# Two graph layers on one core: last 256 columns of e turned by VectorE, last products by halves, tie counts from one scan

## The chip, the cores and the metric

The kernel runs on one core of a Trainium2 chip. Its metric is the device time of one execution in microseconds (us), as the median of three runs. A core has TensorE (PE in the profile; its weight loads are listed as PEld), VectorE (DVE), ScalarE (ACT), GpSimd (POOL) and SyncE (SP), which here issues nearly all DMAs. Each engine executes its own instructions in the order in which they were issued and waits at semaphores for the others.

## The reference

`x` is 3327 x 256, `adj` is 3327 x 3327, everything in float32. Two residual layers are computed.

Layer 0 takes `h = relu(layernorm(x))` and makes two steps (n = 0, 1) with a dense graph and a learned one:

```
R  = (adj + I), rows scaled to sum 1
Xf = Xa = Z0 = h;  Z = 0
for n in (0, 1):
    q, k = Xa W1' W2', Xa W3'
    p = softmax(q k')                      # 3327 x 3327
    A = p, of each row the largest entries until 0.9 of the sum is reached;
        the rest is zero; rows scaled again to sum 1
    Xf = R Xf;  Xa = A Xa
    Z += Xf U1[n]' + Xa U2[n]'
x = x + layernorm(h + Z)
```

Entries that are equal at the border of the 0.9 are kept in the order of their columns. Layer 1 is a graph attention with four heads of 64: `hp = relu(layernorm(x)) W`, scores `leaky_relu(s_i + d_j)` where `adj[i, j] > 0`, softmax over j, product with `hp`, then `x + elu(...)`.

## The kernel before

The 3327 nodes are padded to 26 tiles of 128 (NT = 26, NP = 3328). The whole program is written as pieces of work given to a planner, the class `Plan`. Each piece has an engine, a length in us, a rank (smaller is sooner), the pieces that it needs, and counted buffers that it takes and gives back; `lag` is the time after its end at which others may build on it, for a DMA the time to landing. `Plan.order` simulates the engines with these lengths and lags and writes the instructions out in that order. So a changed length, lag or buffer count changes no computation, but can change the order of issue on every engine.

One **row tile** of attention (52 of them: 26 in each step) goes like this. `logits` (L905) makes q k' in PSUM in pieces of 1024, 1024, 1024 and 255 columns; `exps` (L920) is ScalarE's exponential of each piece into the buffer `e` (128 x 3328). `count` (L959) counts on ScalarE against trial thresholds and GpSimd steps them. `window` (L1017, L1022) takes on VectorE the best eight of each of 16 column pieces as 128 candidates; `sort` and `choose` (L1049 to L1070) find the smallest value kept, and how many entries equal to it are kept: `choose` marks the ties among the candidates (L1062), sums them over the four quarters of the row (L1064, L1065), scans the four sums (L1066), and makes one threshold for each quarter (L1069, L1070). `drop` (L1075) zeroes what lies under the threshold, quarter by quarter: 1024, 1024, 1024 and 255 columns.

The product A Xa needs the tiles of `e` transposed. In 49 of the 52 rows (`BLOCKED`) the first three quarters take this way: `turn_blocks` (L1112) transposes 32 x 32 blocks on VectorE, `put_blocks` (L1116) writes the quarter to DRAM, `get_blocks` (L1121) reads it back in four DMAs with the blocks in their places, and `attend_blocks` (L1128) multiplies eight tiles of it with `rhs` on TensorE. `exps` writes these quarters with pairs of tiles interleaved, for that purpose. The last two tiles, columns 3072 to 3327, are transposed by two TensorE matmuls with the identity (`turn`, L1087) into a PSUM buffer of the pool `px`, copied to SBUF by ScalarE or VectorE (L1098), and multiplied from there (`attend`, L1105). In the other three rows, at the end of step 1, all 26 tiles go that second way. There are two `px` buffers, shared with the projections of `finish1` and `finish2`. Beside the rows, `Full` multiplies adj with main or c (L1153), from tiles `at` that SP loads (L1147): in both steps this fills TensorE between the rows.

**Layer 1** (`attend_neighbours`) is four column blocks b of W = 832 nodes, each over the 26 source tiles j. For every j ScalarE makes a mask (L1751, L1752), VectorE makes four heads of 832 exponents (L1763) in a buffer `e` or `e2`, TensorE makes the products (`product`, L1779, 128 x 64 weights, two heads beside each other) and the denominators (`sums`, L1793, 128 x 32 weights, four heads beside each other); `sums` of two j are put together (`JG = 2`). When the last j is through, ScalarE copies the sums out of PSUM (L1842, L1848), and for each of seven tiles TensorE transposes (L1866), VectorE divides (L1904, L1905), ScalarE makes relu and exp (L1914, L1915), GpSimd adds x (L1918), VectorE joins (L1922) and SP stores (L1925). In the last block nothing else is left to do beside this.

Of the kernel before, what the change touches and what calls it, by code (L numbers as in the profile page):

```python
# [587 lines left out]
def fast(  # L588
# [58 lines left out]
    with ExitStack() as l0:  # L647
# [23 lines left out]
        blocks = spill.tile([3, 4, P, 2 * P], F32, name="blocks")  # L671
# [194 lines left out]
        plan = Plan(dict(rows=1, mvs=3, pl=2, px=2, acca=1, accf=1, et=3, at=4, y=1, e2=3, mask=2, e5=1, qg=2, **BUFS))  # L866
# [4 lines left out]
        class Row:  # L871
# [3 lines left out]
                "b w t0 t1 t2 u g k2 p0 p1 p2 p3 D0 D1 D2 v z r0 s0 s1 s2 h x th tq mid dh kh fl d up h0 h1 room zs cnt "  # L875
# [38 lines left out]
            def exps(self, k):  # L914
                pl = self.pl.pop(k)
                to = self.e[:, PART * k : PART * k + pl.shape[1]]
                if k < 3 and self.i < BLOCKED[self.n]:
                    to = to.rearrange("p (g q t) -> p g t q", g=4, t=2)
                    pl = pl.rearrange("p (g t q) -> p g t q", g=4, t=2)
                S.activation(  # L920
                    to,
                    pl,
                    AF.Exp,
                    accum_out=(self.p0, self.p1, self.p2, self.p3)[k],
                )

            def row_sum(self):
                k = self.NAMES.index("p0")
                S.activation(self.sc[:, k + 4 : k + 8], self.sc[:, k : k + 4], AF.Copy, accum_out=self.s)
# [114 lines left out]
            def choose(self):  # L1044
# [14 lines left out]
                V.scalar_tensor_tensor(out_, win, nxt, keep, ALU.is_gt, ALU.mult, accum_out=self.cnt)  # L1059
                V.tensor_sub(self.m, met[:, 2, i], self.cnt)  # L1060
                ties = small.tile([P, PIECES * 8], F32, name="rest", bufs=1).rearrange("p (c r) -> p c r", r=8)
                V.tensor_scalar(ties, self.cands, nxt, None, ALU.is_equal)  # L1062
                num, upto = (small.tile([P, 4], F32, name=name, bufs=1) for name in ("num", "upto"))
                V.tensor_reduce(num[:, :3], ties[:, :15, :].rearrange("p (a c) r -> p a (c r)", a=3), AX.X, ALU.add)  # L1064
                V.tensor_reduce(num[:, 3:], ties[:, 15, :], AX.X, ALU.add)  # L1065
                V.tensor_tensor_scan(upto, num, num, 0.0, ALU.add, ALU.bypass)  # L1066
                V.scalar_tensor_tensor(num, upto, self.m, num, ALU.is_le, ALU.mult, accum_out=met[:, 4, i])
                self.thr = small.tile([P, 4], F32, name="thr")
                V.tensor_scalar(upto, upto, self.m, 2.0**-24, ALU.is_gt, ALU.mult)  # L1069
                V.tensor_scalar(self.thr, upto, 1.0 - 2.0**-24, nxt, ALU.add, ALU.mult)  # L1070

            def drop(self, o):

                piece = self.e[:, o * PART : min((o + 1) * PART, N)]
                V.scalar_tensor_tensor(piece, piece, self.thr[:, o : o + 1], piece, ALU.is_gt, ALU.mult)  # L1075
# [24 lines left out]
            def attend(self, g):  # L1100
# [3 lines left out]
                for j in range(4 * g, min(4 * g + 4, NT)):  # L1104
                    T.matmul(  # L1105
                        self.acc, et[:, j - 4 * g, :], rhs[self.n][:, j, :], start=(j == 0),
                        stop=j == NT - 1 and self.i >= BLOCKED[self.n],
                    )

            def turn_blocks(self, g):  # L1110
                part = self.e[:, g * PART : (g + 1) * PART].rearrange("p (g s t) -> p g t s", g=4, t=2)
                V.transpose(part, part)  # L1112

            def put_blocks(self, g):
                src = self.e[:, g * PART : (g + 1) * PART].rearrange("p (g w) -> p g w", g=4)
                nc.sync.dma_start(blocks[g].rearrange("g p w -> p g w"), src)  # L1116

            def get_blocks(self, g, o):
                part = slice(o * P // 4, (o + 1) * P // 4)
                src = blocks[g, :, :, o * P // 2 : (o + 1) * P // 2].rearrange("g (b s) w -> s (g b) w", b=4)  # L1120
                nc.sync.dma_start(self.e[part, g * PART : (g + 1) * PART].rearrange("p (c w) -> p c w", w=P // 2), src)  # L1121

            def attend_blocks(self, js, stop):
                for j in js:
# [3 lines left out]
                    T.matmul(self.acc, lhs, rhs[self.n][:, j, :], start=(j == 0), stop=stop and j == js[-1])  # L1128
# [180 lines left out]
        def finish1(row, done, rank):  # L1309
# [73 lines left out]
            y = plan.put("SP", 0.5, r + 0.3, store, needs=[a], give=["ystage"], lag=3.0)  # L1383
# [97 lines left out]
        def failures(n):  # L1481
# [14 lines left out]
            V.tensor_tensor(one, met[:, 4], met[:, 5], ALU.not_equal)  # L1496
# [7 lines left out]
        def search(row, rank, keys, stats_of, fresh):  # L1504
# [4 lines left out]
            for g in range(2):  # L1509
# [8 lines left out]
                for k in (2 * g, 2 * g + 1):  # L1518
                    got.append(
                        plan.put("ACT", 1.15 if k < 3 else 0.5, rank - 2.5, row.exps, k, needs=[a], give=["pl"])  # L1520
# [29 lines left out]
            a = plan.put("DVE", 3.1, rank - 1.0, row.choose, needs=[a, may], take=["cum"])  # L1550
            total = plan.put("POOL", 1.0, rank - 1.0, row.total, needs=[a], give=["cum"])
            drops = []
            for o in range(4):
                a = plan.put(
                    "DVE", 1.07 if o < 3 else 0.4, rank - 1.0, row.drop, o, needs=[a], hold=1.0 if o < 3 else 0.3,
                    lag=0.15 if o < 3 else 1.5,
# [4 lines left out]
        def attention(row, rank, total, drops, right):  # L1561
            a = None
            if row.i < BLOCKED[row.n]:
                come = []
                for g in range(3):
                    b = plan.put("DVE", 1.25, rank - 1.001, row.turn_blocks, g, needs=[drops[g]])
# [5 lines left out]
                last = plan.put("PE", 0.22, rank - 0.01, row.turn, 6, needs=[drops[3]], take=["px"])  # L1572
                last = plan.either(
                    ("ACT", 0.27, row.turned_by_s), ("DVE", 0.39, row.turned_by_v), rank - 2.6, 6, needs=[last],
                    take=["et"], give=["px"],
                )
                for j in (0, 4, 8, 12, 24, 16, 20):
                    if j == 24:
                        a = plan.put("PE", 0.864, rank, row.attend, 6, needs=[last, a], give=["et"])
                        continue  # L1580
                    a = plan.put(
                        "PE", 1.728, rank, row.attend_blocks, range(j, j + 4), j == 20, needs=[come[j // 8], a, right],
# [19 lines left out]
        def full(n, t, rank, right, after):  # L1602
# [3 lines left out]
                plan.put("SP", 0.4, rank, f.load, q, needs=[after], take=["at"], lag=3.3) for q in range(-(-NT // JC))  # L1606
# [20 lines left out]
        def attend_neighbours(rows, ends, done, fulls):  # L1627
# [4 lines left out]
            JG = 2  # L1632
            logits_done = [r.pieces["logits"] for r in rows]
# [73 lines left out]
            for b in range(4):  # L1707
# [13 lines left out]
                group, groups_e = [], []  # L1721
                for j in range(NT):
# [31 lines left out]
                    def exponents(a, j=j, held=held, b=b):  # L1754
                        if a == 0:
# [3 lines left out]
                                if k < 4  # L1759
                                else extra["e"][k - 4]  # L1760
# [11 lines left out]
                    def product(a, j=j, held=held, q=q, open_acc=open_acc):  # L1772
# [3 lines left out]
                        for c in range(2):  # L1776
# [10 lines left out]
                    def sums(j=j, held=held, q=q, open_den=open_den):  # L1787
# [3 lines left out]
                        for c in range(2):  # L1791
# [14 lines left out]
                    else:  # L1806
# [5 lines left out]
                    mine = "e" if j % 7 < 4 else "e2"  # L1812
                    x_ = plan.put(
                        "DVE", 2.0, rank, exponents, 0, needs=[m_, both[0], ends[j][0], more if mine == "e2" else None,
# [3 lines left out]
                    last_e = y_  # L1818
                    x_ = plan.put(
# [6 lines left out]
                    if len(group) == JG or j == NT - 1:  # L1826
# [22 lines left out]

                r1 = r0 + 9.0  # L1850
# [267 lines left out]
```

## Time and profile before

| | |
|---|---|
| time, median of 3 runs | 2105.58 us (2104.02 to 2105.99) |
| profiled execution: time, span | 2100.08 us, 2098.2 us |
| TensorE busy | 2037.8 us (97%), granted clock 0.994 |
| VectorE busy | 1729.7 us (82%) |
| ScalarE busy | 1300.0 us (62%) |
| GpSimd busy | 990.7 us (47%) |
| DMA | 338.56 MB, 580513 packets; the main queue's packets 66.4% of 16 engines' span |

The profile is of one execution; the span runs from its first to its last instruction. Busy time of an engine is the union of its instructions. A group line of the profile gives source line, engine, operation, output and inputs, shape and count, then busy us, mean ns of one, and the idle time ahead of it with what ended it. float32 matmuls appear as two records each; transposes (L1087) as one. Matmul records overlap, so what one costs is read from start to start. The prologue ends at about 95 us, step 0 of layer 0 at about 750 us with leftovers to 840, step 1 at about 1610 us, and layer 1 fills the rest.

### The profile page before, as it was taken

How to read it: one execution, taken by the hardware profiler on the slowest of the kernel's cores; microseconds unless marked ns; L12 is line 12 of the kernel's file. 1: busy time of each engine (PE TensorE's matmuls, PEld its weight loads, DVE VectorE, ACT ScalarE, POOL GpSimd, SP SyncE). 2: the span in 40 equal slices, each digit the busy share in tenths (PEclk: the TensorE clock that was granted, in tenths of full speed). 3: DMA queues.
4: the chain of work that ended last, by engine and by line, in shares of the span. 5: the costliest groups of instructions: out<-in, count | busy, mean ns of one | idle time of the engine just before them, and what ended most of it. 6: DMA issues, size and time to landing. Idle time of an engine off the chain costs nothing. (4 is left out here: it accounts for less than half of the span.)

```text
span 2098.2 us, 34334 instructions
## 1 busy us (share of the span) xinstructions
PE 2037.8 (97%) x10695; PEld 1415.2 (67%) x10695; DVE 1729.7 (82%) x4105; ACT 1300.0 (62%) x2480; POOL 990.7 (47%) x2170
## 2 busy tenths in 40 slices
PE   8999999999999989989999999999999999999997
PEld 6477777878787778767878787787877333333332
DVE  5689897778876871578998979988987999999895
ACT  5767665666556621777778776778652547465552
POOL 4476654446544630567778777777772000000001
PEclk9999999999999999999999999999999999999999
DMA  4188888678877685697787888887743544453341
GB/s 116 45 190 186 194 180 195 168 152 196 189 183 172 176 186 138 199 232 165 181 189 176 203 188 191 185 191 192 182 126 89 157 141 142 125 147 115 112 127 34
DMA packets 580513, 338.56 MB, mean 161 GB/s; under 512 B 327931, under 2 KB 533281, under 8 KB 580321
## 3 DMA queue, kind: packets, MB, share of 16 engines
q1 hardware_dynamic: 579424, 336.06, 66.4%
q8 instruction: 87, 1.43, 0.3%
q14 instruction: 106, 0.86, 0.1%
q10 hardware_dynamic: 896, 0.21, 0.0%
HBM read 242.86 MB, written 93.05 MB: 160 GB/s over the span
## 5 line engine op out<-in xcount | busy, mean ns | idle before, releaser
L959 ACT ACTIVATE junk<-e,sc 128x3327 fp8e5<-128x3327 f32 x147 | 451.0, 3068 | 31.4 <-POOL sc L996 29.8
L1128 PE MATMUL acca<-rhs,e 128*128 128x256 f32 x1872 | 426.8, 381 | 4.6 <-DMA e<-blocks 4.6
L1128 PEld LDWEIGHTS acca<-rhs,e 128*128 128x128 f32 x1872 | 364.9, 197 | 48.7 <-issue 6.0
L1153 PE MATMUL accf<-c,at 128*128 128x256 f32 x1352 | 316.5, 385 | 17.1 <-DMA at<-in_adjt_dram 8.5
L1153 PE MATMUL accf<-main,at 128*128 128x257 f32 x1352 | 313.3, 381 | 5.4 <-ACT main L1304 2.5
L1153 PEld LDWEIGHTS accf<-c,at 128*128 128x128 f32 x1352 | 252.8, 192 | 67.5 <-DMA at<-in_adjt_dram 10.2
L1153 PEld LDWEIGHTS accf<-main,at 128*128 128x128 f32 x1352 | 250.4, 190 | 54.3 <-issue 11.5
L1022 DVE MAX8 cands<-y 128x8 f32<-128x205 f32 (+1 forms) x832 | 242.9, 361 | 3.6
L1918 POOL TENSOR_TENSOR qq<-qq 128x256 f32<-128x256 f32 x4 | 3.0, 759 | 457.0 <-ACT qq L1914 457.0
L1017 DVE SCALAR_TENSOR_TENSOR y<-e,sc 128x1639 f32<-128x1639 f32 x84 | 165.1, 1965 | 62.9 <-POOL sc L1007 61.7
L920 ACT ACTIVATE e<-pl 128x1024 f32<-128x1024 f32 (+1 forms) x168 | 152.9, 920 | 75.4 <-PE pl L905 74.7
L1752 ACT ACTIVATE et<-at 128x448 bf16<-128x448 f32 (+1 forms) x204 | 112.6, 552 | 128.6 <-DVE e L1763 73.3
L1779 PE MATMUL pl<-e,main 128*64 128x416 f32 x1024 | 190.4, 517 | 0.1
L1075 DVE SCALAR_TENSOR_TENSOR e<-e,thr 128x1024 f32<-128x1024 f32 (+1 forms) x168 | 178.4, 1066 | 2.4 <-DMA at<-in_adjt_dram 0.3
L905 PE MATMUL pl<-kt,qg 64*128 64x512 f32 (+1 forms) x832 | 173.7, 536 | 0.4 <-ACT qq L920 0.4
L1112 DVE STREAM_TRANSPOSE e<-e 128x1024 f32<-128x1024 f32 x117 | 146.1, 1248 | 3.7
L1779 PEld LDWEIGHTS pl<-e,main 128*64 128x64 f32 x1024 | 70.3, 137 | 111.0 <-issue 91.5
L1763 DVE SCALAR_TENSOR_TENSOR e<-c,low,et 128x832 f32<-128x832 f32 x128 | 128.8, 1070 | 6.1 <-issue 3.2
L905 PEld LDWEIGHTS pl<-kt,qg 64*128 64x128 f32 x832 | 71.5, 186 | 83.4 <-issue 76.2
L1751 ACT ACTIVATE at<-at 128x448 f32<-128x448 f32 (+1 forms) x204 | 110.8, 543 | 25.7 <-DMA at<-in_adjt_dram 25.6
L1763 DVE SCALAR_TENSOR_TENSOR e<-qq,low,et 128x832 f32<-128x832 f32 x120 | 120.5, 1073 | 4.1 <-PE accf L1793 2.9
L959 ACT ACTIVATE junk<-qq,sc 128x3327 fp8e5<-128x3327 f32 x35 | 107.4, 3068 | 10.7 <-POOL sc L996 10.4
(550 smaller groups left out, 3540.7 us busy)
## 6 DMA issues: line engine op xcount, KB each, us to landing
at<-in_adjt_dram SPq DMA_DIRECT2D x414, 256.0 KB
blocks<-e SPq DMA_DIRECT2D x117, 512.0 KB
e<-blocks SPq DMA_DIRECT2D x468, 128.0 KB
at<-in_adjt_dram SPq DMA_DIRECT2D x102, 192.0 KB
blocks<-qq SPq DMA_DIRECT2D x30, 512.0 KB
qq<-blocks SPq DMA_DIRECT2D x120, 128.0 KB
at<-in_adjt_dram SPq DMA_DIRECT2D x52, 128.0 KB
ys<-ystage SPq DMA_DIRECT2D x26, 256.0 KB
```

The costliest lines, as they stand in the source:

```text
L905: T.matmul(pl[:, lo : lo + m], qg[self.n, self.i // 4][half, self.i % 4, :], kt[half, 512 * k : 512 * k + m], start=True, stop=True,)
L920: S.activation(to, pl, AF.Exp, accum_out=(self.p0, self.p1, self.p2, self.p3)[k],)
L959: S.activation(junk[:, :N], self.e[:, :N], fn, bias=t, scale=-1.0, accum_out=dst, saturate=False)
L1017: V.scalar_tensor_tensor(self.y[:, : hi - lo], self.e[:, lo:hi], self.up, self.e[:, lo:hi], ALU.is_lt, ALU.mult, accum_out=(self.h0, self. ...
L1022: V.max(self.cands[:, a * PIECES // 2 + k, :], self.y[:, at[k] - lo : at[k + 1] - lo])
L1075: V.scalar_tensor_tensor(piece, piece, self.thr[:, o : o + 1], piece, ALU.is_gt, ALU.mult)
L1112: V.transpose(part, part)
L1128: T.matmul(self.acc, lhs, rhs[self.n][:, j, :], start=(j == 0), stop=stop and j == js[-1])
L1153: T.matmul(self.acc[:, : self.w], self.at[j // JC][:, j % JC, :], self.src[:, j, : self.w], start=(j == 0), stop=(j == NT - 1),)
L1752: S.activation(to, src, AF.Sign)
L1763: V.scalar_tensor_tensor(held["e"][:, k, :], extra["both"][b % 2][:, k, :], low[:, j, k : k + 1], held["mask"], ALU.max, ALU.mult,)
L1779: T.matmul(q["acc"][a][k * FH : (k + 1) * FH, c, :C], main[:, j, h * FH : (h + 1) * FH], held["e"][:, h, c * C : (c + 1) * C], start=(j == 0),
```

## The change

1. The last 256 columns of a blocked row take the way of the first three quarters. The third group becomes 1280 columns wide (10 tiles) in `turn_blocks`, `put_blocks`, `get_blocks`; the two TensorE transposes, their copy and `attend` go. `exps` writes the last piece as two strided halves of 128 and 127 columns, with a fifth sum.
2. `choose` takes the number of kept ties from one instruction, scans the 128 tie marks at once, makes 16 thresholds of which `drop` uses four, and makes the tie check (`met[:, 4]`) behind the thresholds; `failures` reads that check in another form.
3. In the last block of layer 1 the last six j (`LATE`) are multiplied by column halves c of 416: first half 0 of all six, then half 1, with the sums of each half behind its products. `leave_half` copies each half out of PSUM; the tiles that lie in half 0 need only that.
4. In the planner: new lengths, lag 7.0 for 3.0 at the `ys` store and 4.0 for 3.3 at the `at` loads, and the buffer tags `e2=3` become `e2=2, ec=1`, by which j = 0, 7, 14, 21 of layer 1 use the space of `c` and the next four the `e` buffers.

```diff
-        blocks = spill.tile([3, 4, P, 2 * P], F32, name="blocks")
+        blocks = spill.tile([NT // 2, P, 2 * P], F32, name="blocks")
...
             def exps(self, k):
...
+                if self.i >= BLOCKED[self.n]:
+                    S.activation(to[:, :m], pl, AF.Exp, accum_out=sums[k])
+                    return
+                to = to.rearrange("p (g q t) -> p g t q", q=P, t=2)
+                if k < 3:
+                    S.activation(to, pl.rearrange("p (g t q) -> p g t q", g=4, t=2), AF.Exp, accum_out=sums[k])
+                else:
+                    S.activation(to[:, 0, 0, :], pl[:, :P], AF.Exp, accum_out=self.p3)
+                    S.activation(to[:, 0, 1, : m - P], pl[:, P:], AF.Exp, accum_out=self.p4)
...
             def choose(self):
...
-                V.scalar_tensor_tensor(out_, win, nxt, keep, ALU.is_gt, ALU.mult, accum_out=self.cnt)
-                V.tensor_sub(self.m, met[:, 2, i], self.cnt)
-                ties = small.tile([P, PIECES * 8], F32, name="rest", bufs=1).rearrange("p (c r) -> p c r", r=8)
-                V.tensor_scalar(ties, self.cands, nxt, None, ALU.is_equal)
-                num, upto = (small.tile([P, 4], F32, name=name, bufs=1) for name in ("num", "upto"))
-                V.tensor_reduce(num[:, :3], ties[:, :15, :].rearrange("p (a c) r -> p a (c r)", a=3), AX.X, ALU.add)
-                V.tensor_reduce(num[:, 3:], ties[:, 15, :], AX.X, ALU.add)
-                V.tensor_tensor_scan(upto, num, num, 0.0, ALU.add, ALU.bypass)
-                V.scalar_tensor_tensor(num, upto, self.m, num, ALU.is_le, ALU.mult, accum_out=met[:, 4, i])
-                self.thr = small.tile([P, 4], F32, name="thr")
-                V.tensor_scalar(upto, upto, self.m, 2.0**-24, ALU.is_gt, ALU.mult)
-                V.tensor_scalar(self.thr, upto, 1.0 - 2.0**-24, nxt, ALU.add, ALU.mult)
+                V.scalar_tensor_tensor(out_, win, nxt, keep, ALU.is_equal, ALU.mult, accum_out=self.m)
+                ties = small.tile([P, PIECES * 8], F32, name="rest", bufs=1)
+                V.tensor_scalar(ties, self.cands.rearrange("p c r -> p (c r)"), nxt, None, ALU.is_equal)
+                V.tensor_tensor_scan(ties, ties, ties, 0.0, ALU.add, ALU.bypass)
+                self.thr = small.tile([P, PIECES], F32, name="thr")
+                V.tensor_scalar(self.thr, ties[:, 7::8], self.m, 2.0**-24, ALU.is_gt, ALU.mult)
+                V.tensor_scalar(self.thr, self.thr, 1.0 - 2.0**-24, nxt, ALU.add, ALU.mult)
+                ends = ties[:, 39:120:40]
+                V.scalar_tensor_tensor(ends, ends, self.m, ends, ALU.is_equal, ALU.mult, accum_out=met[:, 4, i])
...
+            def part(self, g):
+                return self.e[:, g * PART : (g + 1) * PART if g < 2 else NP]
...
             def attention(row, rank, total, drops, right):
...
-                    b = plan.put("DVE", 1.25, rank - 1.001, row.turn_blocks, g, needs=[drops[g]])
+                    b = plan.put(
+                        "DVE", 1.25 if g < 2 else 1.55, rank - 1.001, row.turn_blocks, g, needs=drops[g : g + 1 + g // 2]
+                    )
...
-                last = plan.put("PE", 0.22, rank - 0.01, row.turn, 6, needs=[drops[3]], take=["px"])
-                last = plan.either(
-                    ("ACT", 0.27, row.turned_by_s), ("DVE", 0.39, row.turned_by_v), rank - 2.6, 6, needs=[last],
-                    take=["et"], give=["px"],
-                )
-                for j in (0, 4, 8, 12, 24, 16, 20):
-                    if j == 24:
-                        a = plan.put("PE", 0.864, rank, row.attend, 6, needs=[last, a], give=["et"])
-                        continue
+                for j in range(0, NT - 2, 4):
+                    js = range(j, j + 4 if j < 20 else NT)
...
             def attend_neighbours(rows, ends, done, fulls):
...
+                    if b == 3 and j >= NT - LATE:
+                        for c in range(2):
+                            r = rank if c == 0 else r0 + 9.0
+                            p_ = plan.put("PE", 0.71, r, product, 0, (c,), needs=[x_, last_acc, halves[c]])
+                            p_ = plan.put("PE", 0.71, r, product, 1, (c,), needs=[x_, y_, p_])
+                            halves[c] = plan.put(
+                                "PE", 0.76, r, sums, (c,), needs=[p_, last_den], give=[mine] if c else []
+                            )
+                        continue
...
+                def leave_half(c, q=q):
...
+                    for k in range(2):
+                        S.copy(q["ot"][k][:, c * C : (c + 1) * C], q["acc"][k][:, c, :C])
+                    S.copy(q["ot"][2][:, c * C : (c + 1) * C], q["den"][c][:, :C])
...
                     a = plan.put(
-                        "PE", 0.4, r1 + 0.02, turn, needs=[out_of], take=["px"], give=["y"] * (x0 + P >= W)
+                        "PE", 0.4, r1 + 0.02 if b < 3 else r1 - 0.4, turn,
+                        needs=[out_of if b < 3 else out_half[: 1 + (x0 + m > C)]], take=["px"], give=["y"] * (x0 + P >= W),
                     )
```

## Prediction

> **What bounds the kernel now.** I read the engine totals first, then stretches of 100 us, then the groups of the lines that change, the waits of TensorE, and the end as a timeline.
>
> ```profile
> PE 2037.8 (97%) x10695; PEld 1415.2 (67%) x10695; DVE 1729.7 (82%) x4105; ACT 1300.0 (62%) x2480; POOL 990.7 (47%) x2170
> ```
>
> TensorE is idle for 2098.2 - 2037.8 = 60.4 us of the span. The stretches (columns: stretch, length, busy us and count of PE, PEld, DVE, ACT, POOL, then clock, DMA share, GB/s) show whether that holds in each stage:
>
> ```profile
> 200.00:300.00 100.00, 98.87 (x461) 77.55 (x461) 89.62 (x250) 68.62 (x124) 64.62 (x136) 1.00 0.84 188
> 1300.00:1400.00 100.00, 97.28 (x454) 79.87 (x453) 95.56 (x267) 74.31 (x130) 75.63 (x162) 1.00 0.83 188
> 1700.00:1800.00 100.00, 100.00 (x735) 37.03 (x733) 98.39 (x115) 60.33 (x153) 0.00 (x0) 1.00 0.49 142
> ```
>
> TensorE is the bound in both steps and in layer 1. Close behind are VectorE in step 1 and the DMA engines in both steps. So TensorE work that is taken out is time, as long as these two do not become late. The waits of TensorE are few:
>
> ```profile
> PE accf L1153 <- DMA at<-in_adjt_dram: 10.5, 6, 6.2
> PE px L1087 <- ACT ystage L1347: 8.5, 3, 7.2
> PE acca L1128 <- DMA e<-blocks: 4.6, 6, 1.7
> ```
>
> The second is of the very transposes that go.
>
> **Part 1, the last 256 columns.**
>
> ```profile
> L1087 PE MATMUL px<-ident,e 128*128 128x128 f32 x156 | 27.7, 286 | 8.5 <-ACT ystage L1347 8.5
> L1098 ACT COPY et<-px 128x256 f32<-128x256 f32 x32 | 11.8, 368 | 15.0 <-PE px L1087 10.5 <-PE acca L1105 4.1
> L1098 DVE COPY et<-px 128x256 f32<-128x256 f32 x20 | 8.5, 424 | 30.4 <-PE px L1087 30.3
> L1112 DVE STREAM_TRANSPOSE e<-e 128x1024 f32<-128x1024 f32 x117 | 146.1, 1248 | 3.7
> ```
>
> TensorE: matmul records overlap, so I take start to start. A pair of these transposes moves the next matmul by 0.22 us in 28 cases, by 0.27 in 12, by 0.31 to 0.35 in 7; the mean of these 47 is 0.247 us. 49 blocked rows x 0.247 = 12.1 us less. The products of the last two tiles remain: 217 ns start to start from `et` (L1105) and 224 from `e` with its waits (L1128), so nothing. The ends are 0, if TensorE would have waited there anyhow, and -12.1; I take -12, because in the steps it is busy 97 to 99%.
>
> The wait for `px`: of the 8.5 us, 7.2 are one stall at 744 us, where `px` was held by a copy that waited for a `ys` store. After it the matmuls go at 427 ns instead of 216 for about 3.4 us (granted clock 0.76 in 750 to 760), 1.7 us more. Whoever asks for `px` next, a projection, can stall in the same place; but 49 claims on two buffers fall away, and the longer planned lag of that store puts the copy later in the order. I take half of 8.5 + 1.7, -5; the ends are 0 and -10.
>
> VectorE: the third transpose is a quarter longer, 1248 / 4 = 0.31 us; the `et` copy falls away in 20 of 52 rows, 0.424 x 20 / 52 = 0.16 a row. ScalarE: an extra instruction in `exps` (start to start the 255-column piece takes 0.26 and its accumulator read 0.09; I take two halves at 0.27 each) adds about 0.2 us a row, and 32 copies of 0.37 fall away: even. ScalarE is at 62%, which hides it; without that cover it would be 49 x 0.2 = 10 us.
>
> DMA and SP: no new DMA is issued; each row's third write grows from 512 to 640 KB, and its four reads from 128 to 160 KB.
>
> ```profile
> DMA packets 580513, 338.56 MB, mean 161 GB/s; under 512 B 327931, under 2 KB 533281, under 8 KB 580321
> e<-blocks SPq DMA_DIRECT2D x468, 128.0 KB
> ```
>
> A row adds 512 reads of 256 B (27 ns each in the DMA records) and 128 writes of 1 KB (52 ns): (512 x 27 + 128 x 52) / 16 engines = 1.28 us a row, 5% of a row's 24 us, so the share of 0.83 goes to 0.88. The third group also waits for the fourth `drop` (0.45 us), and lands later. On SP, `at` loads, `ys` stores and query fetches stand behind the third write, which waits for VectorE about 0.45 + 0.31 us longer; four `at` buffers (about 3.5 us of matmuls) hide that. What TensorE lost to DMAs is 10.5 + 4.6 = 15 us in all. I take +4, a quarter more; the ends are 0 and +17 (ten waits of the 1.7 us that the longest `e` wait took). At the end of step 0 the longer way of the last row is partly exposed: +1 (0 to 2).
>
> **Part 2, `choose`.** Out go L1060 (170 ns), L1064 (278), L1065 (151) and L1066 (176): 775 ns. In comes a scan of 128. Scans of 4, 24 and 32 took 166, 207 and 224 ns (medians); about 2 ns an element gives 0.22 + 96 x 0.0021 = 0.42 us, with ends of 0.3 (1 ns) and 0.9 (6 ns, the slope between the means 210 and 258). The other instructions stay in number and width class; the tie check stands ahead of `drop` on VectorE as before. So -0.35 a row, and with part 1 VectorE gets 0.31 - 0.16 - 0.35 = -0.2 us a row, 10 us in all. It is not the bound: 0, ends -4 and +2.
>
> [...]
>
> **Part 3, halves at the end.**
>
> ```profile
> 2065.94 5.81 PE L1779 MATMUL pl<-e,main 128*64 128x416 f32 x32
> 2074.61 3.01 PE L1779 MATMUL pl<-e,main 128*64 128x416 f32 x16
> 2082.46 0.88 PE L1793 MATMUL accf<-c,qd 128*32 128x416 f32 x8
> 2083.86 0.18 DVE L1904 RECIPROCAL rows<-px 128x4 f32<-128x4 f32 x1 [18.77 <-PE px L1866]
> 2088.28 0.16 DVE L1904 RECIPROCAL rows<-px 63x4 f32<-63x4 f32 x1
> 2090.02 1.60 DVE L1922 SCALAR_TENSOR_TENSOR e<-e 128x256 f32<-128x256 f32 x3
> ```
>
> Two j take 2074.61 - 2065.94 = 8.67 us from product to product. Their 32 + 32 records run two and four at once, in 24 slots; a slot inside a run is 0.349 us, so 8.38 us. The rest, 0.29 us, is paid at the two changes between 64 and 32 columns of weights. Six j now have three pairs of changes; by halves they have twelve: 9 x 0.29 = +2.6 us. Three tiles are transposed between products of the second half: 3 x (0.33 us for three transposes + 0.29 for going there and back) = +1.9 us that stood in the tail before. The tail has seven tiles at (2088.28 - 2083.86) / 6 = 0.74 us; three of them leave it: -2.2 us. The first remaining tile now needs the copies of half 1 out of PSUM, about +0.5. Sum +2.8; the ends are -2.2 (changes and transposes cost nothing) and +3.5. VectorE is 18 us ahead there (its last exponents end at 2065.1), so no half waits for it. I take +2.5.
>
> [...]
>
> **Part 4, order.** VectorE may start layer 1 sooner (it is idle from 1610 to 1620), but TensorE is 100% busy there: 0. New lags move pieces in both steps; for that I leave 4 us either way.
>
> **Sum** against the profiled 2100.1 us: -12 - 5 + 4 + 1 + 0 + 2.5 = -9.5, so 2090.6. That execution was 5.5 us under the median of the runs; to the median the sum gives 2105.6 - 9.5 = **2096** us. With the middle of the bounds, 2088 to 2101.
>
> **Rivals.**
> - *DMA becomes the bound* (slower). Everything of a blocked row now comes over DRAM, and TensorE has no product of it without a read. For it: shares of 0.83 over 100 us, stretches of 10 us above 1.0, and the 6.2 us stall on `at` at 901 us. Against: only 15 us lost so far. With the `px` gain gone too, the sum is -12 + 1 + 2.5 = -8.5 plus what DMA costs, so it decides from 8.5 + 4.2 = 12.7 us, about one row in six losing 1.7 us; one row in five (17 us) gives +8.5: 2114. Chance 0.17.
> - *The gain is eaten*: TensorE merely waits where it transposed. -12 - 0 + 8 + 1 + 2.5 = -0.5: 2105. Chance 0.13.
> - *The order gets better throughout*: -12 - 10 + 0 + 0 - 4 + 2.5 = -23.5: 2082. For it: idle TensorE is in a few long stalls that hang on lags which the change raises. Chance 0.15.
> - *Forecast*: 0.55.
>
> **Chances.** About 0.2% (4.2 us) can be told from no change. Faster 0.55 + 0.15 = 0.70, same 0.13, slower 0.17. The range goes from 2083 to 2111: it leaves out about half of the best and half of the worst case.
>
> **What would show it.** L1087 falls from 176 transposes to 78 and L1098 to a few; TensorE busy falls by about 10 us and its idle time stays near 60. L1121 moves 160 KB in a third of its reads, and DMA share in 200 to 300 us rises to about 0.88. The scan takes about 0.42 us. The last `sums` end later than the gain of part 1 alone would put them, and from there to the last join it is about 6.5 us instead of 8.3. I am wrong if waits on `e<-blocks` or `at` grow past 30 us, or if the end by halves takes no extra TensorE time.

## The result and the profile after

| | before | after |
|---|---|---|
| median | 2104.8 us (2103.69 to 2105.99, 4 runs) | 10844.11 us (10840.67 to 10851.86, 4 runs) |
| ratio | | 5.1525 [5.1436, 5.1615] |
| profiled execution: time, span | 2100.08 us, 2098.2 us | 10840.67 us, 10838.9 us |

The forecast of 2096 us is off by a factor of five, and no case that the prediction listed reaches there. Two questions follow: where 8739 us come from, and what the change does to the 2100 us that it was written for.

**The whole.** From the page of after: TensorE's busy tenths in 40 slices, its granted clock in tenths, the chain that ended last, and the costliest group (line, engine, operation, tiles, count, then busy us and mean ns):

```profile
PE   9999999822222222222321333333332222116666
PEclk9999999956666666666665666666666666558998
DVE scr L201 42%; DVE e L440 4%; DVE junk L390 3%; DVE scr L219 3%; DVE e L448 3%; PE acc L260 2%; PE pl L176 2%; DVE scr L223 2%; DVE e L215 2%; DVE e L224 2%; DVE e L444 1%; DVE mx L179 1%; DVE cand L197 1%; DVE cut L207 1%; PE pm L285 1%
L201 DVE SCALAR_TENSOR_TENSOR scr<-e,cand 128x3327 bf16<-128x3327 f32 x1404 | 5124.3, 3684 | 32.1 <-ACT e L182 9.3
```

A slice is 271 us. Through the first seven and most of the eighth TensorE is as busy as before; then another program runs, in which VectorE carries the chain. L201 is not in any function that the prediction spoke of. The timeline of after at the hand-over (start, length, engine, line, operation, tiles):

```profile
2088.08 2.14 DVE L1946 SCALAR_TENSOR_TENSOR e<-e 128x256 f32<-128x256 f32 x3
2089.56 0.20 POOL masks.py:197 MEMSET ident<- 128x128 f32 x1
2090.87 9.23 SPq L128 DMA_DIRECT2D main<-in_x_dram  x13
2093.56 0.43 DVE L92 BATCH_NORM_STATS2 bst<-main 128x6 f32<-128x256 f32 x1 [2.59 <-DMA main<-in_x_dram]
```

L1946 is the last join of the kernel proper (L1922 before); it ends at 2090.2 us. What comes behind it loads x and starts at the first layernorm again. The code says why:

```python
        fast(tc, again, *args)
        with tc.If(tc.nc.values_load(again, min_val=0, max_val=1) > 0):
            general(tc, *args)
```

`fast` holds everything that the prediction weighed, and sets `again` where `failures` finds a row whose selection it can't vouch for; `general` (L59 on) then computes everything once more, by a bisection of every row on VectorE (L201). It takes 10838.9 - 2090 = 8749 us. In before it didn't run: that profile has no row of L201. The first pass ends at 2090.2 us in after against 2091.6 us in before, one execution each: by this the forecast 9.5 us are not there, and the flag decides the time.

**The first pass.** The rows that answer to those of before, from after (stretch, length, busy us and count of PE, PEld, DVE, ACT, POOL, clock, DMA share, GB/s):

```profile
200.00:300.00 100.00, 99.73 (x460) 78.95 (x459) 86.87 (x234) 67.42 (x122) 58.42 (x128) 1.00 0.90 195
1300.00:1400.00 100.00, 98.68 (x456) 79.34 (x456) 91.01 (x229) 76.52 (x134) 78.74 (x166) 1.00 0.89 203
1700.00:1800.00 100.00, 100.00 (x737) 36.66 (x737) 98.24 (x114) 60.15 (x152) 0.00 (x0) 1.00 0.48 141
```

TensorE still carries all three, VectorE has 3 to 5 us less to do in the first two, and there the DMA share rose from 0.84 and 0.83 to 0.90 and 0.89. For sums over the whole pass I take the run *no_tie_flag* (next section), which is after without one condition of the flag and so without `general`. Its engine totals, DMA packets, three of TensorE's waits (total, times, longest) and four groups:

```profile
PE 2032.2 (97%) x10597; PEld 1407.0 (67%) x10597; DVE 1717.7 (82%) x3929; ACT 1294.6 (62%) x2547; POOL 993.9 (47%) x2170
...
DMA packets 611871, 351.39 MB, mean 167 GB/s; under 512 B 353018, under 2 KB 564640, under 8 KB 611680
```

```profile
PE accf L1156 <- DMA at<-in_adjt_dram: 17.5, 9, 8.0
...
PE acca L1131 <- DMA e<-blocks: 5.4, 5, 1.6
...
PE pl L1776 <- DVE c L1760: 3.5, 1, 3.5
```

```profile
L1115 DVE STREAM_TRANSPOSE e<-e 128x1280 f32<-128x1280 f32 x39 | 59.1, 1516 | 4.1
L1064 DVE TENSOR_TENSOR_SCAN rest<-rest 128x128 f32<-128x128 f32 x52 | 22.6, 435 | 1.8
L1067 DVE TENSOR_SCALAR thr<-thr,met 128x16 f32<-128x16 f32 x52 | 12.4, 239 | 1.9
L1087 PE MATMUL px<-ident,e 128*128 128x128 f32 x78 | 12.4, 298 | 4.4 <-DVE e L1075 4.4
```

(Lines behind L1498 have numbers three smaller in this kernel than in after.) The transposes on TensorE went, as the change says, from 156 out of `e` and 20 out of `qq` in before to 78. TensorE is busy 5.6 us less (2037.8 to 2032.2), but idle 2100.5 - 2032.2 = 68.3 us of the span, 7.9 more than the 60.4 of before. It waited 15.1 us for `at` and `e<-blocks` in before and 22.9 us here; the wait for `c` at the start of layer 1 is new.

### The profile page after: what moved, and what is told of

It reads as the page before. It is cut to its first block, busy times and chain, and to the rows that moved or that the text cites. A ratio compares the mean times of both kernels' runs of the same rounds, so it can differ in the third digit from the quotient of the medians.

```text
span 10838.9 us, 68191 instructions
## 1 busy us (share of the span) xinstructions
PE 4877.8 (45%) x21465; PEld 3199.9 (30%) x21465; DVE 10097.1 (93%) x12033; ACT 2860.8 (26%) x4948; POOL 1040.4 (10%) x2281
## 4 chain that ended last, share of the span: by engine, by line
DVE 68%; PE 8%; issue 2%; ACT 1%; another core or an unknown queue 0%; DMA 0%; POOL 0%; ACTq 0%; POOLq 0%; DVEq 0%; SPq 0%
DVE scr L201 42%; DVE e L440 4%; DVE junk L390 3%; DVE scr L219 3%; DVE e L448 3%; PE acc L260 2%; PE pl L176 2%; DVE scr L223 2%; DVE e L215 2%; DVE e L224 2%; DVE e L444 1%; DVE mx L179 1%; DVE cand L197 1%; DVE cut L207 1%; PE pm L285 1%
## 5 line engine op out<-in xcount | busy, mean ns | idle before, releaser
L201 DVE SCALAR_TENSOR_TENSOR scr<-e,cand 128x3327 bf16<-128x3327 f32 x1404 | 5124.3, 3684 | 32.1 <-ACT e L182 9.3
L449 PE MATMUL acc<-e,hp 128*65 128x512 f32 (+1 forms) x1456 | 721.7, 644 | 344.5 <-DVE e L448 344.5
L440 DVE SCALAR_TENSOR_TENSOR e<-both,sd,e 128x512 f32<-128x512 f32 (+1 forms) x728 | 475.2, 728 | 8.6 <-ACT e L439 8.6
L439 ACT ACTIVATE e<-both,dlow 128x512 f32<-128x512 f32 (+1 forms) x728 | 443.8, 678 | 53.6 <-PE acc L449 53.6
L448 DVE SCALAR_TENSOR_TENSOR e<-adjb,e 128x512 f32<-128x512 f32 (+1 forms) x728 | 431.0, 667 | 5.4 <-ACT e L445 5.0
L390 DVE CUSTOM_DVE_ANT_0 junk<-an,db 128x3327 bf16<-128x3327 f32 (+1 forms) x104 | 370.7, 3624 | 2.0 <-ACT db L375 1.2
L219 DVE TENSOR_TENSOR_SCAN scr<-scr 128x3327 uint16<-128x3327 bf16 x52 | 368.5, 7086 | 0.0
L260 PE MATMUL acc<-main,et 128*128 128x257 f32 x1352 | 351.9, 407 | 0.0
L176 PE MATMUL pl<-kt,qt 64*128 64x512 f32 (+1 forms) x728 | 344.6, 614 | 3.2 <-ACT e L177 3.2
L260 PE MATMUL acc<-xa,et 128*128 128x257 f32 x1352 | 343.5, 400 | 3.8 <-ACT et L253 3.8
```

The costliest lines, as they stand in the source:

```text
L176: T.matmul(pl[:, :w], qt, kt[:, c : c + w], start=True, stop=True)
L201: V.scalar_tensor_tensor(junk, e[:, :N], cand[:, g : g + 1], e[:, :N], ALU.is_ge, ALU.mult, accum_out=sums[:, g : g + 1],)
L219: V.tensor_tensor_scan(rank, ties, ties, 0.0, ALU.add, ALU.max)
L260: T.matmul(acc, et[:, j - j0, :], src[:, j, :], start=(j == 0), stop=(j == NT - 1))
L390: V.tensor_tensor_reduce(junk[:p], an[:p], db[:p, k, :N], scale=1.0, scalar=-BIG, op0=ALU.add, op1=ALU.max, accum_out=top[:p, t, k : k + 1],)
L439: S.activation(e[:, k, :w], both[:, 1, k, :w], AF.Identity, bias=dlow[:, j, k : k + 1])
```

## The experiments

Each time stands beside the kernel before on the same chip, whose median there was 2101.58 to 2101.84 us; ratios and differences are to that. Where no ratio is given, it is one run. A letter in an expectation names a theory; each expectation says what its theory gives.

### Why `general` runs

Two theories. Either the new tie check raises the flag by itself, or the products A Xa are now summed in another order (tiles 0 to 25 straight, where before took 24 and 25 ahead of 16 to 23), which changes the rounding of `Xa`, so of the logits of step 1, so which entries are equal at a border.

**no_tie_flag**: after, without the tie condition in `failures`.

```diff
-            V.tensor_scalar(one, met[:, 4], 0.0, None, ALU.is_equal)
-            V.tensor_mul(one, one, two)
-            V.tensor_add(b, b, one)
```

> The changed kernel, with the tie condition (met[:, 4] is 0 while met[:, 5] is not) left out of `failures`; this leaves that one check out, all other flags stay. Theory A (one or a few rows have entries equal to the border value inside one quarter, which one threshold a quarter can't split; the tie condition flags them and `general` does everything again): no second pass, 2103 us, as the first pass of the changed kernel ends its last join at 2090.2 us of the span where the kernel before ended it at 2091.6. Rival B (another condition raises the flag: wrong values from the new way of the last 256 columns, seen as a wrong count, a wrong sum or a score out of reach): 10844 us, no change.

Measured 2101.47 us, 1.000 [0.9988, 1.0012] of before's 2101.58. So it is this one condition, and the first pass of the whole change takes as long as before did.

**tile12_masked**: after, with the flags of row tile 12 of step 1 cleared.

```diff
+            if n == 1:
+                V.memset(b[:, 12:13], 0.0)
```

> The changed kernel with all conditions kept, but the flags of row tile 12 of step 1 set to zero after they are made; this leaves those 128 rows unchecked. Theory A in its narrow form (a single row, in that tile, raises the flag): 2103 us. Rival C (the new tie count or tie check is wrong by itself, so that rows in many tiles raise it) and rival B: 10844 us, as the other 51 tiles still raise it.

2101.47 us: all flags that count are in one tile of 128 rows of step 1.

**old_choose**: after, with `choose`, thresholds and tie check of before.

> The changed kernel with `choose`, the thresholds and the tie condition put back word for word to those of the kernel before (four sums over quarters, four thresholds). Theory A (the tie is in the values, and neither code can split it): 10844 us, within 1%. Rival C (the new tie code miscounts): 2103 to 2125 us, the first pass alone with 0.35 us a row more of VectorE work.

10855.78 us, with the same 1404 instructions of L201. The tie check of before raises the flag as well on what after computes; the new check is not the cause.

**old_order**: after, with the tiles summed in the order of before.

```diff
-                for j in range(0, NT - 2, 4):
-                    js = range(j, j + 4 if j < 20 else NT)
+                for j in (0, 4, 8, 12, 24, 16, 20):
+                    js = range(j, min(j + 4, NT))
...
```

> The changed kernel with only the order of the sums in A Xa put back: the ten tiles of the third group are multiplied as 24, 25, then 16 to 23, as the kernel before does, instead of 16 to 25. Same products, another rounding. Theory A with rounding as its source (the border tie is a coincidence of the last bits of Xa after step 0): the tie goes away, 2103 us. Rival C or B (logic or data wrong whatever the rounding): 10844 us.

2103.49 us, 1.0007 [0.9994, 1.002]: no `general`, though all four parts of the change are there.

**b_natural**: before, with nothing but the order of sums changed.

```diff
-                for j in (0, 4, 8, 12, 24, 16, 20):
+                for j in (0, 4, 8, 12, 16, 20, 24):
...
```

> The kernel before with one edit: the last two tiles of a row are multiplied behind the third group (order 0 to 25) instead of between tiles 15 and 16, as the changed kernel does; they are still transposed by TensorE, and `choose` is the old one. Theory A (the flag comes from the last bits of the values, which follow the order of the sums): it goes through `general` too, about 10844 us. Rival (it is the new way of the last columns, or the new tie code, that makes the flag): 2102 us within 10.

10840.62 us. Its profile has the 1404 instructions of L201 too. This settles it: the order of sums alone costs the factor of five, in the old kernel too. What the profile can't show are the values; rounding is all that this order changes in what is computed. By the condition, in after a row of tile 12 has entries equal at its border of which some must be kept and some dropped, with no quarter's end between them, and `drop` has one threshold for each quarter. That before and old_order have no such row is, by these runs, a matter of rounding with these inputs, and not a property of their order.

### What each part does to the first pass

Starting from old_order, which has the whole change and no flag, parts are put back one after another. The theory in the prediction's words: transposes and `px` give 17 us, the rest takes a few back.

**oo_tags**: old_order with the buffer tags of before (`e2=3`, j = 0 of layer 1 in an `e` buffer again).

```diff
-e2=2, ec=1
+e2=3
...
-mine = ("ec", "e", "e", "e", "e", "e2", "e2")[j % 7]
+mine = "e" if j % 7 < 4 else "e2"
```

> The changed kernel with the old order of the sums (as old_order), and the buffer tags of layer 1 put back: e2=3, j = 0 to 3 in `e` buffers, 4 to 6 in the space of c and rhs. Theory D (the new tags make the first j of layer 1 wait until the last adj product has read c: TensorE stalls 3.5 us on `c` at 1612 us): that stall goes, 3.5 us less than old_order, 2100 us; up to 8 less if the 4.4 us stall ahead of it, on the transposes of the last rows, goes as well. Rival (TensorE is the bound and the work only moves): no change, 2103.5.

2093.45 us, 0.996 [0.9946, 0.9975]: 10.1 us less than old_order, each to its own before, and more than the 3.5 to 8 of its theory. In the profiled executions the wait for `c` (3.5 us), a wait of the last transposes for `drop` (4.4) and 6.6 us of waits for `at` are gone, and a wait of 7.0 us for VectorE (L1019) is new; so the tags are shown as the cause, and the stall on `c` as only a part of it.

**oo_tags_whole**: also the last block of layer 1 in whole columns (part 3 undone).

```diff
-                    if b == 3 and j >= NT - LATE:
+                    if False:
...
```

> As oo_tags, and the last block of layer 1 multiplied whole as in the kernel before (part 3 undone). Theory E (halves cost 3.7 us of TensorE by changes of weight width and by transposes between the products, and save 2.2 us of tail): 1.5 us less than oo_tags, 2098.5. Rival (the halves gain 2.2 us of tail and cost nothing): 2.2 us more than oo_tags.

2091.04 us, 0.9957 [0.994, 0.9973]: 2.4 us less than oo_tags, where its theory gave 1.5; the two intervals overlap.

**oo_tags_whole_lags**: also the lags 3.0 and 3.3 of before; what is left is part 1 and `choose`.

```diff
-lag=7.0
+lag=3.0
-lag=4.0
+lag=3.3
```

> As oo_tags_whole, and the planner's lags of the `ys` store and the `at` loads put back to 3.0 and 3.3; what is left of the change is part 1 and the new `choose`. Theory F (the longer lags took away the stalls of TensorE on px in step 0, 8.5 us in the kernel before, of which none is left): 5 us more than oo_tags_whole. Rival (taking the transposes away did that by itself, and the longer lags only move the waits into step 1, where they grew from 16 to 31 us): no change or up to 5 us less.

2088.81 us, 0.9947 [0.9928, 0.9967]. I had expected the old lags to cost 5 us; they gave 2.2, though the intervals of this step and the last overlap.

From the other side, one part at a time on before:

**part1_only**: the last 256 columns by VectorE, summed in the old order; `choose`, lags, tags and the end as before.

> The kernel before with part 1 alone: the last 256 columns over VectorE and DRAM, the old order of the sums, old `choose`, old tags, old lags, last block whole. Theory G (the forecast's first term: 49 pairs of transposes, 12 us of TensorE, come off the time nearly whole): 2101.7 - 11 = 2091. Rival H (the gain of 12.8 us that oo_tags_whole_lags showed comes in good part from `choose`, as VectorE is up to 95% busy in step 1): 2097 or more.

2110.65 us, 1.0042 [1.0028, 1.0056]. The part that the forecast rested on makes the kernel slower by 8.8 us. From its page and its waits:

```profile
PE 2038.4 (97%) x10597; PEld 1410.5 (67%) x10597; DVE 1736.9 (82%) x4087; ACT 1290.8 (61%) x2547; POOL 991.2 (47%) x2170
...
PE accf L1159 <- DMA at<-in_adjt_dram: 22.1, 13, 5.5
```

The wait for `at` was 10.5 us in before. And TensorE is not busy for less: 2038.4 us, where it was 2037.8 with the transposes.

**b_new_choose**: the new `choose`, with its planned length of 2.65 for 3.1, and nothing else.

> The kernel before with part 2 alone: one scan of the 128 tie marks, 16 thresholds, tie check behind the thresholds, and the planner's length 2.65 for 3.1 of it. Theory G (VectorE is not the bound): within 3 us of 2101.7. Rival H: 2097 or less.

2088.43 us, 0.9944 [0.9924, 0.9963]. The part that I put at zero gives 13.4 us.

**b_new_tags**: the new tags and nothing else.

> The kernel before with the new buffer tags of layer 1 alone (e2=2, ec=1; j = 0, 7, 14, 21 in the space of c). Theory D (the first product of layer 1 can't start before the last adj product of layer 0 has read c, and TensorE has nothing else to do there): 4 to 10 us more, 2106 to 2112. Rival (the tags cost only together with the longer chain of part 1): within 2 us of 2101.7.

2106.36 us, 1.002 [1.0009, 1.0031]: 4.5 us slower. The timeline of TensorE in it shows a place where:

```profile
1607.91 11.39 PE L1153 MATMUL accf<-c,at 128*128 128x256 f32 x52
1622.79 4.59 PE L1779 MATMUL pl<-c,main 128*64 128x416 f32 x15 [3.49 <-DVE c L1763]
```

and the same place in before:

```profile
1590.94 1.62 PE L1779 MATMUL pl<-e,main 128*64 128x416 f32 x8
...
1619.05 4.41 PE L1779 MATMUL pl<-e,main 128*64 128x416 f32 x24
```

The exponents of the first j stand in the space of `c`, and are written only when the last product of adj with `c` is through, at 1619.30 us. In before the first eight products of layer 1 stood between the last rows of step 1, from `e`, and the rest followed the last product with `c` at once; now TensorE runs dry for 3.49 us at the seam.

### Where part 1's 12 us went, and where `choose`'s 13 come from

`choose` can gain by VectorE's time or, since its planned length changed, by the order in which the planner writes everything. Part 1 can lose by the DMA that it adds, or by falling into a bad order.

**choose_old_order**: the new `choose`, planned at the old 3.1. **order_only**: before, planned at 2.65, no instruction changed (its edit is shown). **part1_order**: part1_only, planned at 2.65.

```diff
-            a = plan.put("DVE", 3.1, rank - 1.0, row.choose, needs=[a, may], take=["cum"])
+            a = plan.put("DVE", 2.65, rank - 1.0, row.choose, needs=[a, may], take=["cum"])
```

> The kernel before with the new `choose` alone, and the planner left in the belief that it takes 3.1 us, so that every engine gets its instructions in the order of the kernel before. Theory I (VectorE's time counts: `choose` takes 2.62 instead of 3.19 us a row, rows come sooner and TensorE waits less): about 2090, as b_new_choose. Theory J (the 13 us of b_new_choose come from another order of issue): 2101.8 within 3.

2095.17 us, 0.9966 [0.9955, 0.9978]: between the two theories; 6.5 us of the gain are there without the new order.

> The kernel before with one number changed: the planner is told 2.65 instead of 3.1 us for `choose`, which goes on taking 3.19 us. No instruction changes, only their order. Theory J: about 2089, as b_new_choose. Theory I: 2101.8 within 3, or more, as rows come later than planned.

2097.64 us, 0.9979 [0.9969, 0.9989]: the number given to the planner is worth 4.0 us by itself. The two add up to 10.5 of the 13.4 us; 3 us come only with both, or lie within the intervals.

> As part1_only (old `choose` of 3.19 us), but the planner is told 2.65 us for it, which gives the order of oo_tags_whole_lags. Theory J (part1_only is late only by its order): about 2089, as oo_tags_whole_lags. Theory I (part 1 loads VectorE and DMA, and what `choose` gives back pays for it): 2105 or more.

2100.29 us, 0.9997 [0.9986, 1.0008], between the 2089 and the 2105 of its theories. Against order_only part 1 costs 2.7 us, against before in the old order 8.8, and on top of the new `choose` (oo_tags_whole_lags against b_new_choose, each to its own before) 0.6, which lies within the intervals. In none of three orders does it gain.

The clock granted to TensorE goes along with this. Its mean over all executions was 0.9947 in order_only and 0.9946 in b_new_choose, 0.9934 in choose_old_order and 0.9916 in part1_only, beside 0.9928 or 0.9929 in before. Taken times 2100 us, as an estimate, that is 3.8 of the 4.0 us of order_only, 3.8 of the 13.4 of b_new_choose, 1 of the 6.5 of choose_old_order, and 2.5 of the 8.8 that part 1 loses. In the profile of before the clock is under 0.95 in five of the 200 stretches of 10 us from 90 on, all at TensorE's three longest waits or just behind them: 0.90 and 0.76 from 740 and 750 us (7.2 us for `ystage`), 0.75 and 0.91 from 900 and 910 (6.2 us for `at`), and 0.83 from 1560 (3.4 us for L1164). So by the estimate a good part of what an order of issue is worth would come through the clock; no run changes the clock alone.

**more_dma**: b_new_choose, which keeps the TensorE transposes, with about the traffic of part 1 added to each blocked row: 128 KB written behind the third quarter, and 128 KB moved from DRAM to DRAM in 256-byte pieces behind its last read.

```diff
...
                 nc.sync.dma_start(blocks[g].rearrange("g p w -> p g w"), src)
+                if g == 2:
+                    nc.sync.dma_start(extra_out, ident.unsqueeze(1).to_broadcast([P, 2, P]))
...
+                if (g, o) == (2, 3):
+                    nc.sync.dma_start(extra_in[:, :, :DA], extra_out.rearrange("p t (a d) -> p (t a) d", d=DA))
```

> b_new_choose with the transposes kept, and beside each blocked row's third write a further write of 128 KB and behind its last read a further transfer of 128 KB in pieces of 256 bytes from DRAM to DRAM, of data that nothing uses, unknown to the planner: the traffic that part 1 adds, without part 1. Theory K (the 12 us of TensorE that part 1 takes out are lost again to the added traffic): 8 to 12 us more than b_new_choose, 2096 to 2100, by waits of TensorE on `at` and `blocks`. Rival L (they are lost because the last tiles of a row now come late, and no longer lie ready): 2088 within 3.

2110.96 us, 1.0042 [1.003, 1.0053], so 22.5 us more than b_new_choose (22.7 with each to its own before): the direction of the theory that DMA eats the 12 us, and a size above the 8 to 12 that it gave. The main queue's packets took 0.671 x 2086.5 = 1400 us of the 16 engines in b_new_choose, and here:

```profile
q1 hardware_dynamic: 618624, 348.91, 69.4%
```

0.694 x 2105.3 = 1461 us, so 61 us or 1.25 us a row. Part 1's own traffic was estimated at 1.28 us a row; by the same reckoning it is 0.703 x 2086.8 = 1467 us in oo_tags_whole_lags, 67 us or 1.37 a row. The experiment isn't an exact copy: it issues two more DMAs a row on SP, where part 1 makes existing ones longer, and the planner doesn't know of them. And its waits are not those of the theory alone:

```profile
PE accf L1157 <- DMA at<-in_adjt_dram: 15.6, 10, 5.0
PE px L1087 <- ACT ystage L1351: 9.3, 4, 4.2
...
PE acca L1132 <- DMA e<-blocks: 2.7, 2, 1.6
```

Beside b_new_choose (its lines follow) the waits for `at` and `blocks` grew by 7.1 us, less than the transposes cost, and the wait of the transposes for `ystage` by 5.8, which a kernel with part 1 doesn't have. So the run shows that added traffic of this size delays TensorE by more than the transposes cost; it doesn't give the price of the same traffic in part 1.

What part 1 costs is seen in the waits of TensorE. b_new_choose, without part 1:

```profile
PE accf L1151 <- DMA at<-in_adjt_dram: 9.7, 8, 5.3
...
PE px L1085 <- ACT ystage L1345: 3.5, 3, 1.8
...
PE acca L1126 <- DMA e<-blocks: 1.5, 1, 1.5
...
PE px L822 <- DMA qg<-kqs: 0.7, 1, 0.7
```

oo_tags_whole_lags, with it:

```profile
PE accf L1156 <- DMA at<-in_adjt_dram: 10.8, 7, 4.7
PE acca L1131 <- DMA e<-blocks: 9.1, 13, 1.7
...
PE px L822 <- DMA qg<-kqs: 4.6, 1, 4.6
```

The waits shown that a DMA ended go from 11.9 to 24.5 us: 12.6 us more; the 3.5 us for `ystage` went. TensorE is busy 2036.0 - 2027.5 = 8.5 us less, idle 2086.8 - 2027.5 = 59.3 us of the span where it was 2086.5 - 2036.0 = 50.5, and the spans are 0.3 us apart. Whether a row's tiles came later because the DMA queues were fuller, or because their write started later, behind the fourth `drop`, no run separates.

## Why the prediction was wrong

**The step that failed first** is not in the sum at all. The prediction read the new loop in `attention` as one that removes `turn` and `attend`, and never as one that moves tiles 24 and 25 from ahead of 16 to 23 to the end of a float32 sum. It also read `failures` as a changed form of the same check, without asking what is done with its answer. So a second pass stood in the sum at nothing, without a reason; the runs showed 8739 us for it. The trace can't show a branch that wasn't taken, but a function of four hundred lines (`general`, L59 to L469) has no row in before's profile, and that was to be seen. A second computation of the same 52 row tiles and the same layer 1, priced by the only thing there is to go by, the kernel itself at 2100 us, would have come to some 4200 us in all, far below what it took. Its chance could not have been worked out from the profile, but it belonged among the rivals, with its condition. Of the prediction's signs several came true (78 transposes, a scan of 435 ns, 6.0 us from the last sums to the end), and the waits on `e<-blocks` and `at` stayed under its 30 us (22.9); none of them watched the flag.

**The sum for the first pass** was -9.5 us; measured is 0 (1.000 [0.9988, 1.0012]). From the experiments, each step to its own before (the order of sums is old_order against no_tie_flag):

| step | predicted | measured |
|---|---|---|
| `choose` and its planned length | 0 | -13.4 |
| part 1 on top of it | -12 - 5 + 4 + 1 = -12 | +0.6 (alone: +8.8) |
| new lags | 0 | +2.2 |
| last products by halves | +2.5 | +2.4 |
| new tags | 0 | +10.1 (alone: +4.5) |
| order of sums (old to straight) | not seen | -2.0 |
| sum | -9.5 | -0.1 |

The steps of 0.6, 2.2, 2.4 and 2.0 us lie within overlapping intervals. That the first pass comes so near to no change, as in the rival "The gain is eaten", is luck: -13.4 and +10.1, both put at nothing, cancel.

- *Part 1, TensorE*: the cost is right. The transposes of L1087 go from 24.1 to 10.2 us start to start in after, or from 21.6 without the three of before that stand ahead of gaps of 0.6 to 1.1 us; 12.1 was worked out. That this is time, as TensorE is busy 97 to 99%, is what failed.
- *Part 1, `px`*: the waits of L1087 on `ystage` are gone from no_tie_flag, but a wait of L1087 on `drop` (4.4 us) takes their place; in oo_tags and oo_tags_whole_lags both are gone. So whether the 5 us come hangs on the tags and the order, and in the whole change they did not.
- *Part 1, DMA*: +4 was the term of part 1 that was mis-sized. I scaled the 15 us of DMA waits by a quarter; measured are 12.6 us more beside b_new_choose, and 11.6 more for `at` alone in part1_only. The share of 0.88 that I forecast for 200 to 300 us came out at 0.90. Against the 12 us of the transposes this leaves no gain, the case of the rival "The gain is eaten"; "DMA becomes the bound" had the cause, but asked for 12.7 us and more to call the kernel slower.
- *Part 1, VectorE*: the transpose of 1280 columns takes 1516 ns against 1248, +0.27 where 0.31 was worked out. Less the 0.16 of the copies that is 0.1 us a row; at what VectorE's time was worth in part 2 about 1 us in all, an estimate that no run tests alone.
- *Part 2*: the scan takes 435 ns, predicted 420. `choose` as a whole went from 3.19 to 2.62 us a row (medians), -0.57 where I had -0.35. Start to start on VectorE, the second threshold costs 143 ns after and 287 before, though its own duration is 239 and 249 ns: behind it stands now the tie check, which doesn't need its result, and starts before it is through. I added durations of single instructions, where the chain of dependent ones pays from start to start. The larger error was "it is not the bound: 0". With VectorE 82% busy overall and 96% in the stretch from 1300 us, half a microsecond in each row was worth 6.5 us with the order unchanged. In that run's profiled execution TensorE is idle 2094.1 - 2037.4 = 56.7 us, where it was 60.4.
- *Part 3*: right in sum, as far as the runs can tell. Undone, it gives 2.4 us back. In the profile it is seen by its parts: layer 1's products take 301.4 us start to start in before and 304.3 in no_tie_flag (one wait of 1.1 us left out), its sums 1.1 more, and the tail is shorter. From the timeline of after, the last sums, the first and the last division:

```profile
2083.33 0.91 PE L1793 MATMUL accf<-e,qd 128*32 128x416 f32 x8
...
2085.23 0.18 DVE L1928 RECIPROCAL rows<-px 128x4 f32<-128x4 f32 x1 [9.65 <-PE px L1890]
...
2087.13 0.16 DVE L1928 RECIPROCAL rows<-px 63x4 f32<-63x4 f32 x1
```

  From the end of the sums at 2084.2 to the end of the last join at 2090.2 it is 6.0 us; 6.5 was predicted and 8.3 had been before.
- *Part 4*: "TensorE is 100% busy there: 0" failed for the tags. The prediction looked at whether VectorE would start layer 1 sooner, and not at who still reads the space that j = 0 was given. The lags were within the 4 us that I had left for them; a lag that is nearer to the truth isn't worth anything by itself.

The two fastest kernels are b_new_choose (2088.43 us) and oo_tags_whole_lags (2088.81 us); the first has one part of the change and no new traffic.

## What to carry to other kernels

Where a kernel has a fast path with a check behind it, a changed order of float32 sums is a change of its input to that check: look for the branch, price the slow path, and count it as a rival. Work that was taken off the bounding engine and put on DMA queues at a share of 0.81 to 0.82 (b_new_choose, 100 to 700 and 960 to 1500 us) came back here as waits, 8.5 us less busy and 8.8 more idle; compare the waits of that engine with and without the part, and see what ends each of them when you test the traffic by itself. Where a planner writes the order, take every part alone and with the planner's numbers alone: here a changed length with no changed instruction was worth 4 us, as much as the smaller parts.

## What the runs showed of the hardware

- About 1.25 us of added packet time a row, spread over 16 DMA engines at a share of 0.81, with two more DMAs a row, cost 22.5 us over 49 rows, 0.46 us a row (more_dma against b_new_choose).
- Pieces of 256 bytes took 27 ns and pieces of 512 bytes 28 ns in the DMA records of before (means), that is 0.105 and 0.055 ns a byte. Part 1's reads add pieces of 256 bytes: packets under 512 bytes went from 327931 in before to 353018 in no_tie_flag, 512 for each of 49 rows.
- In `choose` of after, the second [128 x 16] threshold of 239 ns held back the next instruction, which doesn't need its result, by 143 ns; the first, whose result the next one needs, by 270 ns (medians, start to start).
